# First layer of a macaron block: tokens loaded transposed as well, mean taken out by a constant product, reciprocal deviation put into the gates, order written out

## The chip, the cores and the metric

One core of one Trainium2 chip runs the whole kernel. The time is that of one execution on the device in microseconds (us), all of the kernel in one launch; of several runs the median counts. TensorE (PE) multiplies matrices, VectorE (DVE), ScalarE (ACT) and GpSimd (POOL) work on tiles in the core's own memory, SyncE (SP) issues the DMAs. Each engine takes its instructions in one fixed order and waits for other engines on semaphores.

## The reference

1024 tokens of 512 numbers pass three layers, all in float32:

```
x = x + 0.5 * FFN(LN(x));  x = x + Attention(LN(x));  x = x + 0.5 * FFN(LN(x))
LN(x) = (x - mean) / sqrt(var + 1e-5)
FFN(y): scores = y Wr^T (64 experts); gates = softmax of the 16 highest, others 0
        h = y A^T (64 experts x 16); out = (h * gate) B * 2
```

The attention has 32 heads over four sequences of 256 tokens, causal, and takes most of the time. The change concerns the first FFN.

## The kernel before, in words

The tokens lie in eight tiles of 128; two tiles make a pair. The first FFN, `ffn("f1", late=True)` from L274, works pair by pair in a fixed rhythm of generators. For a pair, `prepare` (L312) takes mean and variance on VectorE (`norm_stats`, L88), the root on ScalarE (L97), the reciprocal on VectorE (L101), writes the normed tile on ScalarE (L111), and turns it with eight 128x128 transposes on TensorE (`turned_x`, L114, ptx_f), which ScalarE copies to fxT_f (L321). Then come sums of quarters of it on VectorE (fxs_f, L171), the routing product against wr_sb (pr_f, L338) and `gates` (L282): the two highest groups of eight, an exponential on ScalarE (L301) and a division.

`hidden` (L348) multiplies a pair with A, `back` (L455) the gated result with B. Both are written as seven products of quarter matrices (Strassen's scheme, `seven`, L197) whose results are added on VectorE or copied on ScalarE (L367 to L371). Sums of quarters of A and B (at_f, bt_f; L191) are made once, on VectorE and POOL. `gated` (L378) multiplies the hidden values by their gates on POOL; `turned` (L409) turns the result with four groups of four transposes (pth_f, L441) and copies (L442). Pair 2's is turned by VectorE's 32x32 transposes and DMAs instead (`move`, L390), and ScalarE copies what comes back (L418). `back` adds to x on VectorE.

What sets the order: the program makes its calls in an order of its own, and a scheduler places the instructions on each engine from that; only the few marked `keep_in_program_order` are bound. The hidden products of pairs 0 and 1 are interleaved; from pair 2 on, the hidden products of one pair alternate with the back products of the pair before. SP's queue loads x0, x1, wr, two blocks of a, x2, x3, two blocks of a, x4 to x7, b, the first attention weights (L705 to L720, L227 to L250). Beside the pairs POOL makes sums of the attention's weights (L653). The normed tokens for the attention (`norm_pair`, ptx_a) are made behind each pair's back products. TensorE is kept busy from the start by 14 products of zeros (L86). The second FFN uses the same functions with `late=False`.

Of the kernel before, what the change touches and what calls it, by code (L numbers as in the profile page):

```python
# [14 lines left out]
P = 128  # L15
# [12 lines left out]
EPS = 1e-5  # L28
MASKED = -1e30
# [4 lines left out]
def macaron_kernel(  # L34
    ctx: ExitStack,
    tc: tile.TileContext,
    x_in: bass.AP,
    wq: bass.AP,
# [31 lines left out]
    load_x((0, 1))  # L70
    wr_sb = const.tile([P, DC, E], F32, tag="wr", name="wr_sb")
    nc.sync.dma_start(wr_sb, wr_t.rearrange("(c p) e -> p c e", p=P))
# [4 lines left out]
    nc.gpsimd.memset(eps, EPS)  # L77

    warm = const.tile([P, 1], F32, tag="warm", name="warm")
    nc.scalar.activation(warm, eps, AF.Sqrt)  # L80

    zeros = const.tile([P, P], F32, tag="zeros", name="zeros")
    nc.vector.memset(zeros, 0.0)
    idle = ps_s.tile([P, 512], F32, tag="s", name="idle")
    for _ in range(14):
        nc.tensor.matmul(idle[:, 0:P], lhsT=zeros, rhs=zeros, start=True, stop=True)  # L86

    def norm_stats(ts, name):  # L88
# [7 lines left out]
        std = small.tile([P, n], F32, tag="std", name=f"std_{name}")  # L96
        nc.scalar.activation(std, mv[:, :, 1], AF.Sqrt, bias=eps)  # L97
        minus = small.tile([P, n], F32, tag="minus", name=f"minus_{name}")
        nc.scalar.mul(minus, mv[:, :, 0], -1.0)
        rstd = small.tile([P, n], F32, tag="rstd", name=f"rstd_{name}")  # L100
        nc.vector.reciprocal(rstd, std)  # L101
# [5 lines left out]
    def normed(pool, ts, name, made=None):  # L107

        made = made or [pool.tile([P, D], F32, tag="xn", name=f"xn_{name}_{t}") for t in ts]
        for t, xn, (rstd, bias) in zip(ts, made, norm_stats(ts, f"{name}_{ts[0]}")):  # L110
            nc.scalar.activation(xn, x[:, t, :], AF.Identity, bias=bias, scale=rstd)  # L111
        return made
# [114 lines left out]
    def load_experts(scope, name, side, eng, between):  # L227
# [7 lines left out]
        at = pool.tile([P, 3, 2, 512], F32, tag="at", name=f"at_{name}")  # L235
        for i, kn in enumerate(((0, 0), (1, 0), (1, 1), (0, 1))):
            c, e = a_block(*kn)
            nc.sync.dma_start(a_sb[:, c, e], a_v[:, c, e])
            if i % 2:
                between(i // 2)  # L240
        for k in range(2):
            c = slice(4 * k, 4 * k + 4)
            nc.sync.dma_start(b_sb[:, c, :], b_v[:, c, :])
        every = [(k, n) for k in range(2) for n in range(2)]
# [4 lines left out]
        def keep():  # L249
# [6 lines left out]
            lambda: right_sums(eng, a_t3, *a_of, late=nc.gpsimd),  # L256
            lambda: right_sums(nc.gpsimd, b_t3, *b_of),
# [16 lines left out]
    def ffn(name, pairs, a_sums, b_sums, after, late, aside=None):  # L274


        with ExitStack() as scope:
# [4 lines left out]
            def gates(n, ps):  # L282
# [29 lines left out]
            def prepare(pair):  # L312
# [21 lines left out]
                gate = []  # L334
                for i, t in enumerate(pair):
                    ps = ps_mm.tile([P, 512], F32, tag="mm", name=f"pr_{name}_{t}")
                    for c in range(DC):
                        nc.tensor.matmul(  # L338
                            ps[:, :E],
                            lhsT=xt[:, i, c, :],  # L340
                            rhs=wr_sb[:, c, :],
                            start=(c == 0),
                            stop=(c == DC - 1),
                        )
                    gate.append(gates(f"{name}_{t}", ps))
                gated_by.append(gate)

            def hidden(pair, left, hgs):  # L348
# [14 lines left out]
                def read(r, ps):  # L363
# [4 lines left out]
                    elif adds:  # L368
# [4 lines left out]
                steps = STEPS_LATE if late and pair in pairs[:2] else STEPS  # L373
                if late and pair == pairs[1]:
                    steps = [steps[i] for i in (0, 1, 2, 4, 3, 5, 6)]
                yield from seven(product, read, f"ph_{n}", steps)
# [13 lines left out]
            def move(pair, hg):  # L390
# [5 lines left out]
                for i in range(2):  # L396
# [4 lines left out]
                    for t in range(4):  # L401
# [3 lines left out]
                        )  # L405
                for i in range(2):
                    nc.sync.dma_start(hg[:, i], moved[:, i].rearrange("p t x -> p (t x)"))

            def turned(pair, hg):  # L409
                n = f"{name}_{pair[0]}"  # L410
                hs = work.tile([P, 3, 4, P], F32, tag="hs", name=f"hs_{n}", bufs=1)
                if pair in by_dma:
# [3 lines left out]
                    s1, s2, s4 = (hs[:, i] for i in range(3))  # L416
                    for i in range(2):
# [4 lines left out]
                    for to, a, b, op in (  # L422
# [6 lines left out]
                    return {  # L429
                        "M1": a11, "M2": a12, "M3": s4, "M4": a22, "M5": s1, "M6": s2, "M7": a21  # L430
                    }
# [3 lines left out]

                for i, j in ((0, 0), (1, 0), (1, 1), (0, 1)):
                    pool, tag = (ps_t, "pt") if i or j else (ps_s, "s")
                    pt = pool.tile([P, 4, P], F32, tag=tag, name=f"pth_{n}_{i}_{j}")
                    for c in range(4):
                        cc = j * 4 + c  # L440
                        nc.tensor.transpose(pt[:, c, :], hg[:, i, cc * P : (cc + 1) * P], ident)  # L441
                    nc.scalar.copy(hgT[:, i, j * 4 : j * 4 + 4, :], pt)  # L442
# [8 lines left out]
                return {  # L451
                    "M1": a11, "M2": a12, "M3": s4, "M4": a22, "M5": s1, "M6": s2, "M7": a21
                }
# [26 lines left out]
            tokens = prepare(pairs[0])  # L480
            take(tokens, 1)
            yield
            take(tokens, 1)
            yield
            if late:
                second = prepare(pairs[1])
                take(second, 1)
            take(tokens, 1)
            a_right = a_sums()
            for u in range(n + 1):  # L490
                if u == 1 and late:
                    hid = ahead
                else:
                    hid = hidden(pairs[u], lefts[u], hgs) if u < n else iter(())
                tokens = prepare(pairs[u + 1]) if u + 1 < n else iter(())
                behind = after(work, pairs[u - 2]) if u > 1 else iter(())
                if u == 0 and late:

                    take(hid, 3)
# [1174 lines left out]
```

## Time and profile before

| | |
|---|---|
| median of 3 runs | 1114.08 us (1113.94 to 1115.47) |
| span of the profiled execution, first to last instruction | 1112.0 us |
| what the median has beyond that span | 2.1 us |
| TensorE busy | 1101.3 us, 99% |
| VectorE, GpSimd, ScalarE busy | 819.4, 626.1, 439.8 us |
| first hidden product of the first FFN starts | 10.23 us |
| first product of the attention starts | 126.53 us |

No time of the profiled execution other than its span is listed, so the median stands beside it. In the rows of the profile "L354" is a line of the kernel above, "ph_f<-a_f,fxT_f" what is written and read, "x8" the number of records, of which a matmul here has two and a transpose one. The brackets at a row's end give how long the engine stood idle ahead of it and which instruction ended that. TensorE's stretches list what it did; a chain of waits follows the last instruction back to what released it.

### The profile page before, as it was taken

What the parts mean: (1) busy time and instruction counts of PE and PEld (TensorE: products, weight loads), DVE (VectorE), ACT (ScalarE), POOL (GpSimd) and SP (SyncE); (2) the same over time, 40 slices, a digit from 0 to 9 for tenths busy, and PEclk for the clock granted to TensorE, in tenths of its full rate; (3) what the DMA queues carried; (4) which work ended last, traced back from release to release, by engine and by line L of the source; (5) the groups of instructions that cost most, each with busy time, mean ns of one, the idle gap of its engine ahead of it and who ended that gap; (6) DMA issues with size and microseconds to landing.
All of it is one profiled execution on the core that took longest, in us unless ns stands there. A gap on an engine that the chain in (4) does not pass through costs nothing.

```text
span 1112.0 us, 21021 instructions
## 1 busy us (share of the span) xinstructions
PE 1101.3 (99%) x6770; PEld 970.0 (87%) x6770; DVE 819.4 (74%) x2242; ACT 439.8 (40%) x1320; POOL 626.1 (56%) x870
## 2 busy tenths in 40 slices
PE   9999999999999999999999999999999999999998
PEld 6666888899999999999999999999899999995667
DVE  4554677678778778778778878878888978866543
ACT  4453424444544544544544544444452000106410
POOL 4814588736887887788788778878632000002120
PEclk9999999999999999999999999999999999999999
DMA  9221120157756756756656656756798998752331
GB/s 329 93 70 45 29 68 11 33 143 202 204 140 182 203 159 182 204 149 185 204 154 183 197 162 169 212 151 184 204 325 304 346 337 261 253 200 77 96 94 39
DMA packets 203774, 188.45 MB, mean 169 GB/s; under 512 B 74128, under 2 KB 166032, under 8 KB 203408
## 3 DMA queue, kind: packets, MB, share of 16 engines
q1 hardware_dynamic: 203664, 187.11, 56.2%
q8 instruction: 54, 0.88, 0.3%
q14 instruction: 56, 0.46, 0.1%
HBM read 117.18 MB, written 69.86 MB: 168 GB/s over the span
## 4 chain that ended last, share of the span: by engine, by line
PE 90%; DVE 3%; POOL 2%; ACT 1%; issue 1%; DMA 1%; SPq 0%; POOLq 0%; DVEq 0%
PE po_M L1196 15%; PE pqk_c L772 8%; PE po_f L461 8%; PE pqk_b L772 8%; PE pqk_d L772 8%; PE ph_f L354 7%; PE pa L1297 5%; PE ps L1221 5%; PE pv_c L871 5%; PE pqk_a L772 4%; PE pv_b L871 4%; PE ps L1220 2%; PE pa L1304 2%; PE pv_d L871 2%; PE pv_e L871 2%; PE pv_a L871 2%
## 5 line engine op out<-in xcount | busy, mean ns | idle before, releaser
L384 POOL TENSOR_TENSOR hg_f<-hg_f,gate_f 128x512 f32<-128x512 f32 x32 | 35.6, 1124 | 254.4 <-ACT gate_f L309 151.3
L1196 PE MATMUL po_M<-or_M,ol_M 128*128 128x128 f32 x1456 | 164.7, 275 | 0.0
L1196 PEld LDWEIGHTS po_M<-or_M,ol_M 128*128 128x128 f32 x1456 | 163.7, 192 | 0.1
L653 POOL TENSOR_TENSOR wqk_M<-wqk_M 128x128 f32<-128x128 f32 x320 | 141.5, 457 | 12.1
L653 POOL TENSOR_TENSOR wqk_M<-wqk_M,wqk_M 128x512 f32<-128x512 f32 (+1 forms) x64 | 107.1, 1683 | 45.4 <-DMA wqk_M<-in_wkv 16.5
L789 DVE TENSOR_TENSOR qk<-qk,pqk_d 128x512 f32<-128x512 f32 x210 | 116.3, 559 | 20.7 <-PE pqk_d L772 16.8
L1241 ACT ACTIVATE s<-s,least 128x128 f32<-128x128 f32 (+1 forms) x256 | 114.1, 448 | 40.5 <-DVE least L1229 35.6
L1259 ACT ACTIVATE pn<-s,arden 128x128 f32<-128x128 f32 x220 | 94.1, 428 | 47.7 <-DVE arden L1250 43.3
L772 PE MATMUL pqk_c<-xop,wqk_M 128*128 128x256 f32 x448 | 111.4, 380 | 0.1
L772 PE MATMUL pqk_d<-xop,wqk_M 128*128 128x256 f32 x420 | 108.2, 381 | 1.2 <-DVE qk L789 1.1
L772 PE MATMUL pqk_b<-xop,wqk_M 128*128 128x256 f32 x420 | 102.9, 379 | 0.0
L1096 DVE TENSOR_TENSOR ol_M<-ol_M 128x512 f32<-128x512 f32 x104 | 77.3, 744 | 22.6 <-DMA ol_M<-left 21.8
L1229 DVE CUSTOM_DVE_ANT_0 s<-ps,mask 128x128 f32<-128x128 f32 (+1 forms) x256 | 80.9, 353 | 16.3 <-PE ps L1221 12.3
L789 DVE TENSOR_TENSOR qk<-qk,pqk_c 128x256 f32<-128x256 f32 (+1 forms) x112 | 59.5, 531 | 40.5 <-PE pqk_c L772 36.4
L1311 ACT COPY attn<-pa 128x256 f32<-128x256 f32 x128 | 47.4, 371 | 100.6 <-PE pa L1304 87.9
L772 PEld LDWEIGHTS pqk_c<-xop,wqk_M 128*128 128x128 f32 x448 | 79.0, 191 | 8.7 <-ACT qk L821 1.2
L789 DVE TENSOR_TENSOR qk<-qk,pqk_b 128x512 f32<-128x512 f32 x105 | 71.4, 680 | 20.7 <-PE pqk_b L772 19.9
L772 PEld LDWEIGHTS pqk_b<-xop,wqk_M 128*128 128x128 f32 x420 | 74.9, 191 | 7.5
L772 PEld LDWEIGHTS pqk_d<-xop,wqk_M 128*128 128x128 f32 x420 | 73.0, 191 | 9.1 <-DVE qk L789 2.9
L1297 PE MATMUL pa<-pT,vbuf 128*128 128x256 f32 x256 | 76.4, 380 | 0.8 <-ACT pT L1287 0.5
L1221 PE MATMUL ps<-qk 128*128 128x256 f32 x256 | 76.5, 380 | 0.0
L653 POOL TENSOR_TENSOR wv_M<-wv_M 128x128 f32<-128x128 f32 x160 | 70.6, 458 | 3.8
(192 smaller groups left out, 2355.0 us busy)
## 6 DMA issues: line engine op xcount, KB each, us to landing
ol_M<-left SPq DMA_DIRECT2D x52, 512.0 KB, 5.6
moved<-s SPq DMA_DIRECT2D x440, 48.0 KB, 1.8
pT<-moved SPq DMA_DIRECT2D x110, 192.0 KB, 2.9
wv_M<-in_wkv SPq DMA_DIRECT2D x64, 128.0 KB, 2.7
wqk_M<-in_wq SPq DMA_DIRECT2D x64, 128.0 KB, 2.3
wqk_M<-in_wkv SPq DMA_DIRECT2D x64, 128.0 KB, 2.5
wo<-in_wo SPq DMA_DIRECT2D x16, 512.0 KB, 4.6
left<-attn SPq DMA_DIRECT2D x16, 512.0 KB, 3.3
```

Of the source, the lines that this page charges most:

```text
L354: nc.tensor.matmul(ps, lhsT=left[m][:, c, :], rhs=a_right[m][:, c, :], start=first and c == 0, stop=c == 1, skip_group_check=True,)
L461: nc.tensor.matmul(ps[:, 0:256], lhsT=left[m][:, c, :], rhs=b_right[m][:, c, :], start=first and c == 0, stop=c == 3, skip_group_check=True,)
L653: return nc.gpsimd.tensor_tensor(to, a, b, ALU.subtract)
L772: nc.tensor.matmul(ps[:, i * S : (i + 1) * S], lhsT=right[m][n], rhs=xop[OUTER[m]][:, INNER[n]], start=first and i == 0, stop=True, skip_g ...
L789: nc.vector.tensor_tensor(to, of, ps, ALU.add)
L871: nc.tensor.matmul(ps[:, i * S + t * P : i * S + (t + 1) * P], lhsT=xop[OUTER[m]][:, INNER[n], t * P : (t + 1) * P], rhs=right[m][n], star ...
L1196: nc.tensor.matmul(banks[at // 2][:, cols : cols + P], lhsT=lhsT, rhs=rhs, start=k % 4 == 0 and g == 0 and at % 2 == 0 and t == 0, stop=Tr ...
L1221: nc.tensor.matmul(ps[:, P : 3 * P], lhsT=qT[:, P : 2 * P], rhs=kT, start=True, stop=True)
L1229: nc.vector.tensor_tensor_reduce(out=s[:, cols], in0=ps[:, cols], in1=mask_f[:, cols], scale=-SCALE, scalar=-TAKEN, op0=ALU.add, op1=ALU.m ...
L1241: nc.scalar.activation(s[:, cols], s[:, cols], AF.Exp, bias=least[:, i : i + 1], scale=-1.0, accum_out=den[:, i : i + 1],)
L1259: nc.scalar.mul(pn[:, :, i : 2 * i + 1, :].rearrange("p k t c -> p t k c"), s[:, cols].rearrange("p (t k c) -> p t k c", k=4, c=32), rden[ ...
L1297: nc.tensor.matmul(po[:, 0 : 2 * P], lhsT=v_of(p, j, 2 * b), rhs=of[:, 0:2], start=True, stop=False,)
```

## The change

The host gives the tokens a second time, transposed (x_t, one block per pair). The first FFN loads these raw and takes the mean out of them: for pair 0 by eight matmuls with a constant 1/512 whose result VectorE subtracts, for the others by a diagonal matrix of the means from VectorE, one 128x256 matmul and one subtraction. Routing and hidden products take the tokens without the mean but not divided by the deviation; the reciprocal deviation goes into the exponential's scale and into the gates. It is computed by an addition on VectorE and a power of -0.5 on POOL, also for the attention's pairs 0 and 1; the root stays for its pairs 2 and 3 and for the second FFN.

With that, transposes, copies and normed tiles of the first FFN go. Five products of the constant stand where 14 of zeros stood. SP's queue now has pair 0 transposed, the four blocks of a, x2, x3, pair 1 transposed, x0, x1, wr, b, x4 to x7, the attention's first weights, pair 2 transposed, the stores of a and b, pair 3 transposed. The sums of a and b are split between VectorE and POOL. The order on TensorE, VectorE, ScalarE and POOL through the first FFN is written out: a clock counts TensorE's time (`goes_on`), and work of other engines is put in when its time comes (`later`). Pair 0's hidden products now come first, alone; then those of pair 1, which alternate with the back products of pair 0 in the same way as later pairs. The cut diff:

```diff
     wr_sb = const.tile([P, DC, E], F32, tag="wr", name="wr_sb")
...
 
...
+    halves = const.tile([P, 2], F32, tag="halves", name="halves")
...
 
...
-    zeros = const.tile([P, P], F32, tag="zeros", name="zeros")
-    nc.vector.memset(zeros, 0.0)
-    idle = ps_s.tile([P, 512], F32, tag="s", name="idle")
-    for _ in range(14):
-        nc.tensor.matmul(idle[:, 0:P], lhsT=zeros, rhs=zeros, start=True, stop=True)
-
...
+    nc.scalar.activation(warm, eps, AF.Exp)
+
+    every = const.tile([P, P], F32, tag="every", name="every")
+    nc.vector.memset(every, 1.0 / D)
+    idle = ps_t.tile([P, 512], F32, tag="pt", name="idle")
+    for _ in range(5):
+        nc.tensor.matmul(idle[:, 0:P], lhsT=every, rhs=every, start=True, stop=True)
+
...
+        if whole == "root":
+            std = small.tile([P, n], F32, tag="std", name=f"std_{name}")
+            nc.scalar.activation(std, mv[:, :, 1], AF.Sqrt, bias=eps)
+            nc.vector.reciprocal(rstd, std)
+        else:
+            nc.vector.tensor_scalar_add(rstd, mv[:, :, 1], EPS)
+            nc.gpsimd.tensor_tensor(rstd, rstd, halves[:, 0:n], ALU.pow)
+        if whole is None:
+            return mv, rstd
         minus = small.tile([P, n], F32, tag="minus", name=f"minus_{name}")
         nc.scalar.mul(minus, mv[:, :, 0], -1.0)
-        rstd = small.tile([P, n], F32, tag="rstd", name=f"rstd_{name}")
-        nc.vector.reciprocal(rstd, std)
+        if not whole:
+            return minus, rstd
         bias = small.tile([P, n], F32, tag="bias", name=f"bias_{name}")
...
             c, e = a_block(*kn)
             nc.sync.dma_start(a_sb[:, c, e], a_v[:, c, e])
-            if i % 2:
-                between(i // 2)
+            between(i)
         for k in range(2):
             c = slice(4 * k, 4 * k + 4)
             nc.sync.dma_start(b_sb[:, c, :], b_v[:, c, :])
+        between(4)
...
 
         return (
-            lambda: right_sums(eng, a_t3, *a_of, late=nc.gpsimd),
-            lambda: right_sums(nc.gpsimd, b_t3, *b_of),
+            lambda: right_pieces(a_t3, *a_of),
+            lambda: right_pieces(b_t3, *b_of),
...
+                gate, den, rden = each("gate", E, 4), each("den"), each("rden")
+                for i, ps in enumerate(scores):
+                    nc.vector.scalar_tensor_tensor(
+                        gate[i],
+                        left2[i],
+                        TAKEN,
+                        ps[:, E : 2 * E],
+                        ALU.is_equal,
+                        ALU.mult,
+                        accum_out=den[i],
+                    )
+                for i in range(2):
+                    nc.vector.reciprocal(rden[i], den[i])
+                for i in range(2):
+                    nc.vector.tensor_scalar(
+                        gate[i], gate[i], rden[i], rstd[:, i : i + 1], ALU.mult, ALU.mult
+                    )
+                gated_by.append(gate)
...
+            def prepare_raw(pair):
+
+                n = f"{name}_{pair[0]}"
+                xt = raw(pair)
+                mv, rstd = norm_stats(pair, n, None)
+                diag = work.tile([P, 2, P], F32, tag="mean", name=f"diag_{n}")
+                for i in range(2):
+                    nc.vector.tensor_scalar(
+                        diag[:, i], ident, mv[:, i, 0:1], float(D), ALU.mult, ALU.mult
+                    )
+                yield
+                ps = ps_s.tile([P, 512], F32, tag="s", name=f"pm_{n}")
+                mean = ps[:, 0 : 2 * P].rearrange("p (j t) -> p j t", j=2)
+                nc.tensor.matmul(mean, lhsT=every, rhs=diag, start=True, stop=True)
+                yield
+                nc.vector.tensor_tensor(
+                    xt, xt, mean.unsqueeze(2).to_broadcast([P, 2, DC, P]), ALU.subtract
+                )
+                xs = work.tile([P, 4, 2, P], F32, tag="fxs", name=f"fxs_{n}")
+                lefts.append(left_of(xt, xs))
+                yield
+                for scores in route(pair, xt):
+                    yield
+                yield from gates(pair, scores, rstd)
...
+                for c in range(DC):
+                    nc.tensor.matmul(
+                        ps[:, 0:P], lhsT=every, rhs=firsts["xt"][:, i, c], start=c == 0, stop=c == DC - 1
+                    )
+                return ps
...
+            def first_tile(i, ps):
+
+                to = firsts["xt"][:, i]
+                nc.vector.tensor_tensor(
+                    to, to, ps[:, 0:P].unsqueeze(1).to_broadcast([P, DC, P]), ALU.subtract
+                )
...
-                    steps = [steps[i] for i in (0, 1, 2, 4, 3, 5, 6)]
-                yield from seven(product, read, f"ph_{n}", steps)
+                steps = STEPS_LATE if late and pair == pairs[0] else STEPS
+                def later(r, ps):
+                    reads.append(lambda: read(r, ps))
+
...
-                if u == 1 and late:
-                    hid = ahead
-                else:
-                    hid = hidden(pairs[u], lefts[u], hgs) if u < n else iter(())
-                tokens = prepare(pairs[u + 1]) if u + 1 < n else iter(())
+                a_right, pieces = a_sums()
+                xt = firsts["xt"] = raw(pairs[0])
+                written_out = ExitStack()
+                written_out.enter_context(tc.manual_schedule(engines=FRONT))
+                means = [first_mean(pairs[0], i) for i in range(2)]
+                for i in range(2):
+                    first_tile(i, means[i])
+                xs = work.tile([P, 4, 2, P], F32, tag="fxs", name=f"fxs_{name}")
+                left = left_of(xt, xs)
+                lefts.append(left)
+                reads = []
+                hid = hidden(pairs[0], left, hgs, reads)
+
+                def readings(n):
+                    for _ in range(n):
+                        reads.pop(0)()
+
+                routed = route(pairs[0], xt)
+                take(hid, 3)
+                readings(1)
+                pieces[0](nc.vector)
+                take(hid, 1)
+                pieces[1](nc.vector)
+                readings(2)
...
+                readings(1)
+                scores = next(routed)
+                readings(2)
+                rstd = norm_stats(pairs[0], f"{name}_0", None)[1]
+                take(hid, 1)
+                readings(1)
+                take(routed, 1)
+                take(tokens, 2)
+                take(hid, 1)
+                readings(1)
+                made = gates(pairs[0], scores, rstd)
+                later(0.6, take, made, 2)
+                later(2.2, take, made, 1)
+                b_right, pieces = b_sums()
+                for i, piece in enumerate(pieces):
+                    later(1.5 + 1.2 * i, piece, (nc.gpsimd, nc.vector)[i % 2])
+                later(2.5, lambda: gate_of(0))
+                clock[0] = 0.0
...
+                        for _ in range(k):
+                            goes_on(next(turning_u, 0.0))
+
+                    later(clock[0] + 0.1, take, behind, 1)
+                    if pairs[u - 1] in by_dma:
+                        later(clock[0] + 2.0, turns, 1)
+                    for i in range(7):
+                        take(hid, 1)
+                        goes_on(1.72)
+                        if i == 2 and u == 1:
+                            routing(own)
+                        if i == 5:
+                            later(clock[0], take, tokens, 1)
+                        if i == 3 and u > 1:
+                            take(behind, 1)
+                            goes_on(0.9)
+                            later(clock[0] + 4.0, take, behind, 1)
+                        if pairs[u - 1] not in by_dma:
+                            turns({3: 3, 4: 2}.get(i, 0))
+                    later(clock[0] + 0.8, gate_of, u)
+                    if pairs[u] in by_dma:
+                        moving = move(pairs[u], hgs[pairs[u]])
+                        for at in (5.4, 7.2, 9.0):
+                            later(clock[0] + at, take, moving, 1)
+                    if u == 1:
+                        aside(later, clock[0] + 1.0)
+                    steps = back(pairs[u - 1], left, b_right)
+                    for i in range(7):
+                        take(steps, 1)
+                        goes_on(1.72)
+                        if i == 1 and u + 1 < n:
+                            take(tokens, 1)
+                            later(clock[0] + 0.5, take, tokens, 1)
+                            goes_on(0.43)
+                        if i == 4 and u + 1 < n:
+                            routing(tokens)
+                    take(steps, 1)
+                behind = after(work, pairs[n - 2])
+                left = {}
+                for step in turned(pairs[n - 1], hgs[pairs[n - 1]], left):
+                    goes_on(step)
+                later(clock[0] + 1.5, take, behind, 1)
+                steps = back(pairs[n - 1], left, b_right)
+                for i in range(7):
+                    take(steps, 1)
+                    goes_on(1.72)
+                    if i == 4:
+                        take(behind, 1)
+                        goes_on(0.9)
+                take(steps, 1)
+                goes_on(100.0)
+                written_out.close()
+            else:
+                tokens = ready(pairs[0])
+                take(tokens, 1)
+                yield
+                take(tokens, 1)
+                yield
+                take(tokens, 1)
+                a_right = a_sums()
...
-        experts = load_experts(
-            scope, "f1", "right", nc.vector, lambda i: load_x(range(4, NT) if i else (2, 3))
...
+        def between(i):
+            if i == -1:
+                for k in (0, 2):
+                    nc.sync.dma_start(
+                        raw_tile((0, 1))[:, 0, k : k + 2], xt_in[0][:, 0, k : k + 2]
+                    )
+                nc.sync.dma_start(raw_tile((0, 1))[:, 1], xt_in[0][:, 1])
+            elif i == 4:
+                load_x(range(4, NT))
+            elif i == 3:
+                load_x((2, 3))
+                nc.sync.dma_start(raw_tile((2, 3)), xt_in[1])
+                load_x((0, 1))
+                nc.sync.dma_start(wr_sb, wr_t.rearrange("(c p) e -> p c e", p=P))
+
...
+        def beside(later, time):
+            ones = [one for name in FIRST_SUMS for one in weights["v", 0][2][name]]
+            for i, one in enumerate(ones):
+                later(time + 0.7 * i, one)
+            later(time, experts[2])
```

## The prediction

> **What bounds the kernel now.** I read the busy shares first, then the chain of work that ended last, then TensorE's timeline over the first layer, then what feeds it.
>
> ```profile
> PE 1101.3 (99%) x6770; PEld 970.0 (87%) x6770; DVE 819.4 (74%) x2242; ACT 439.8 (40%) x1320; POOL 626.1 (56%) x870
> PE 90%; DVE 3%; POOL 2%; ACT 1%; issue 1%; DMA 1%; SPq 0%; POOLq 0%; DVEq 0%
> ```
>
> The reader is to see that TensorE is the bound, nearly everywhere. So the change is worth what it takes from TensorE's own work, from its standstills, and from the time before its first useful product. After the first layer both kernels issue the same instructions in the same order on every engine, but for one pair of attention matmuls put 5 us earlier; whatever the first layer gains or loses therefore arrives at the end as a shift.
>
> ```profile
> 1.05 5.71 PE L86 MATMUL idle<-zeros 128*128 128x128 f32 x28 [1.05 <-DVE zeros L83]
> 7.09 1.27 PE L118 MATMUL ptx_f<-ident,xn_f 128*128 128x128 f32 x8 [0.33 <-ACT xn_f L111]
> 8.39 2.00 PE L338 MATMUL pr_f<-wr_sb,fxT_f 128*128 128x64 f32 x16
> 10.23 3.65 PE L354 MATMUL ph_f<-a_f,fxT_f 128*128 128x512 f32 x8
> ...
> 16.45 1.10 PE L354 MATMUL ph_f<-at_f,fxs_f 128*128 128x512 f32 x2 [0.85 <-DVE gate_f L304]
> ...
> 45.54 1.99 PE L461 MATMUL po_f<-b_f,hgT_f 128*128 128x256 f32 x8 [0.84 <-ACT hgT_f L442]
> ...
> 56.01 3.60 PE L354 MATMUL ph_f<-a_f,fxT_f 128*128 128x512 f32 x8
> ...
> 126.53 0.61 PE L871 MATMUL pv_a<-wv_M,xop 128*128 128x128 f32 x4
> ```
>
> Columns: start, us, line, x records. This is TensorE in the first layer: warm-up, transposes, routing, first hidden product at 10.23, third pair's hidden from 56.01, first attention product at 126.53. I set these three marks against the changed order. One product of the seven takes 1.72 (8 records in 3.65 are two of them), four transposes 0.44, routing of a tile 0.86, a 128x256 matmul 0.43. By these rows 10.23 to 56.01 holds 43.2 us of work and 2.6 of standing still; 56.01 to 126.53 holds 69.0 and 1.5.
>
> ```profile
> 42.04 0.58 ACT L442 COPY hgT_f<-pth_f 128x512 f32<-128x512 f32 x1 [1.56 <-PE pth_f L441]
> 42.65 1.28 ACT L301 ACT_TABLE_LOAD   x1
> 43.94 0.55 ACT L301 ACTIVATE pr_f<-sc_f,nmax_f 128x64 f32<-128x64 f32 x2
> 44.44 1.05 ACT L442 COPY hgT_f<-pth_f 128x512 f32<-128x512 f32 x2
> ```
>
> On ScalarE the exponential's table load stands ahead of the copy that TensorE's 0.84 at 45.54 waits for. It is the only one of the eight loads of the front that a standstill of TensorE ends on.
>
> **The change, part by part.** All sums are against the profiled execution: span 1112.0, and the median 1114.08 lies 2.1 above, which I add at the end.
>
> *Start.* The five warm-up matmuls are 10 records 0.213 apart: until 3.2. The mean's eight matmuls need the transposed tile; x0 (256 KB, first in the queue) landed at 3.4, so 3.0 to 3.5. Before, records came 0.213 apart until about 5.6 and 0.111 apart after, though the granted clock stands at 1.00 in the rows throughout. The first tile's mean is 8 records, until 5.1; the second's until 6.0 (half of it at the fast spacing) or 6.8 (none). VectorE's subtraction of 128x512 out of PSUM (0.68 by the addition of L367) ends at 5.9. The first block of a needs 1.0 MB through a queue that had moved 1.1 MB when it landed at 8.1 before: 5.9 to 6.6. First hidden product: 6.1 to 6.8, I take 6.4 against 10.23, 3.8 earlier. But two routings (1.7) that were done by then are now still to come.
>
> *TensorE's work.* Gone after 10.23 are 24 transposes, 8 for each of pairs 1 to 3 (0.87 a pair); new is one 128x256 mean matmul for each (0.43). From the first product to the third pair's: 43.2 + 1.7 - 2 x 0.87 + 2 x 0.43 = 44.0. From there to the attention: 69.0 - 0.87 + 0.43 = 68.6.
>
> *Standstills that go.* 0.85 at 16.45 (VectorE had the second sum of a, 1.20 us, behind the landing at 13.75): the last block of a now lands some 3.4 earlier, since x2, x3 and wr go behind it, and its sums start at about 10.4; at most 0.3 stays. 0.84 at 45.54: no load stands there any more.
>
> *Standstills that come.* Routing weights are now behind 4 MB; at the 390 GB/s of the queue's later stretch they land at 15 to 16 and the first routing is due at 15: 0 to 1.0. The gates of pair 0 on POOL (4 x 1.06) end at about 30.7, the first transposes of its products are due at 30: 0 to 0.5. I take 0.8 in all. Third pair at 6.4 + 44.0 + 0.8 = 51.2, against 56.01.
>
> In the second stretch pair 2's gated products are moved by DMA:
>
> ```profile
> 74.59 1.25 DVE L397 STREAM_TRANSPOSE hgB_f<-hg_f 128x1024 f32<-128x1024 f32 x1 [0.80 <-POOL hg_f L384]
> 73.36 4.25 SPq L402 DMA_DIRECT2D moved_f<-hgB_f  x8
> 77.86 3.56 SPq L407 DMA_DIRECT2D hg_f<-moved_f  x2
> ```
>
> From the second transpose's end (75.84) to the last landing (about 85.0) are 9.2. In the written order the transposes come behind a 128x1024 subtraction (1.23) and four sums (0.4 each) of pair 3, and end 11.5 after pair 2's hidden products; the products are back at 21.3 (the landing takes 3.9 of it). ScalarE has the two copies that wait for them (L559 of the changed kernel, 1.04 each by L418) ahead of the copy (0.58) that frees pair 3's hidden accumulator, and TensorE's fifth product of pair 3 waits for that: due 22.2 (14.4 of back products, four of 1.72, 0.87 of transposes), freed 23.4 with a handover, a standstill of 1.2. The last pair's fourth transpose group waits for a PSUM buffer's copy: 0.45. To these I add 0.8 of small waits, of some 2 that the trace of before has without names, since in-order queues keep such. Second stretch: 68.6 + 2.45 = 71.05, end at 122.3, 4.2 ahead of 126.53.
>
> *Edits at nothing.* ScalarE loses 16 copies and activations and five table loads of 1.28; beyond the one named, it idled, and gains TensorE nothing. The sums of a and b, split between VectorE and POOL: POOL's six of 2.37 ran from 16.38 to 30.5; now four, with VectorE taking the others at 1.2. Cover: VectorE works 26.6 of the 45.8 us; without it each sum of a would cost its 1.2. The transposed tokens are 2 MB more in SP's queue and b lands some 5 us later, but its first product is due at 37. The stores of a and b now stand in SP's queue ahead of pair 3's transposed tokens, which are due 25 us later. The attention's first weight loads wait for the same late products of pair 3 in both; POOL's sums on them ended at 117.3, 9.2 before their use, and shift along. The Sqrt load for the attention's third pair comes early, ahead of an instruction that waits anyway.
>
> *pow on POOL, 128x2, six times:* no row shows it. Below: a memset of 128x1 (0.10); above: 128x1024 (2.37). Nearest in size is the memset; I take 0.3. Each goes ahead of gates or of xop: the first two have 3 us and more of slack, the one for attention pair 0 1.5, the one for pair 3 stands ahead of pair 2's gating, thus on the move above. At 2.37 they would cost 0 + 0 + 0.9 + 2.1 + about 0.5 = 3.5.
>
> *Skill, table loads.* The trace has 1.28 for a load, and the next activation starts 0.01 later. The Trainium skill ("ScalarE: Activation LUTs", What ACT_TABLE_LOAD costs) adds a drain of about 1.4, 2.7 a switch. By that five switches fewer would free 13 us of ScalarE instead of 6.4; for the time it makes no difference, and the row decides.
>
> *Skill, clock.* The spacing above halves at 5.6, 4.5 after the first matmul. The Trainium skill ("TensorE: Matmul & The Clock Gate", What's actually happening) has a free-running window of about 3.4 us that must be filled with activity; it speaks against five warm-up matmuls with gaps behind them. By it the first products could run at half speed until 9.8, a loss of 1.7.
>
> **Rivals.**
>
> A, more: the 1.2 and the unnamed 0.8 do not come, and wr lands in time. Lead 4.2 + 2.0 + 0.5 = 6.7: 1107.4. For it: TensorE's stretches of before stand still only 4%. Against: ScalarE's order is fixed.
>
> B, swallowed. The first products run cold, at 0.213 spacing for the 4.5 us that before needed (half of 4.5 = 2.2), or pow is slow (up to 3.5): lead 0.7 to 2.0, about 1112.6. For it: gaps between warm-up and first product that before did not have. Against: before, the fast spacing came at 5.6 and held through gaps of 0.33.
>
> C, slower. The written order ties pair 3's hidden products to pair 2's move: ScalarE cannot pass the L559 copies, and every us that the move is late is a us of TensorE. Price one for one. Lead is 4.2 with a landing at 21.3 after pair 2's products; it is gone if the landing is at 25.5, and 2.2 slower than before at 27.7, that is, if VectorE's transposes end at 18 instead of 11.5. For it: they stand behind gating on POOL, sums and gates in one fixed queue. Against: VectorE is half idle there (38 of 70.5). About 1117.
>
> D, nothing moves: the first layer ends earlier, but POOL's or the DMA's attention weights pace the rest. Against: the 9.2 of slack, which shifts too. Would give about 1113.5.
>
> **How the numbers follow.** Forecast 0.62, A 0.12, B and D 0.16, C 0.10. The likeliest: 1112.0 - 4.2 + 2.1 = 1109.9; its own range is 1108.3 to 1111.8. About 0.2% (2.2 us) is what a measurement here can tell from no change, so faster means under 1111.85. Faster 0.62 + 0.12 = 0.74, within 0.16, slower 0.10. The range takes in A and half of B: 1106.8 to 1113.6.
>
> **What would show it.** First hidden product at 6.1 to 6.8; its first products 1.72 each, not 3.4; third pair's hidden from 51 to 51.5; a standstill of about 1 at pair 3's fourth hidden step, ended by ScalarE; first attention product at 122 to 122.7; the rest as long as before. I am wrong if the pow rows are over 1 us, if the clock is late, if a wait that I put at nothing shows in TensorE's list, or if the stretch behind the first layer has another length.

## The result, and the profile after

The changed kernel takes 1119.28 us (median of 5, 1117.26 to 1121.69) against 1115.20 in the same series (5, 1113.94 to 1115.81): 1.0041 times as long, 95% interval 1.0028 to 1.0054. It is slower, by 0.4%; I forecast 1109.9 and gave slower a chance of 0.10. The profiled execution is the fastest of the five, 1117.26, with a span of 1115.5.

Shares of the page, and TensorE's timeline (start, us, line, then the idle time ahead of a row and who ended it):

```profile
PE 1098.6 (98%) x6742; PEld 967.5 (87%) x6742; DVE 836.8 (75%) x2260; ACT 419.7 (38%) x1275; POOL 627.2 (56%) x875
PE 89%; DVE 5%; POOL 2%; DMA 1%; issue 1%; ACT 1%; SPq 0%; POOLq 0%; DVEq 0%
```

```profile
6.98 1.96 PE L490 MATMUL ph_f<-a_f,fxT_f 128*128 128x512 f32 x4 [0.95 <-DMA a_f<-in_a_t]
...
20.38 1.96 PE L490 MATMUL ph_f<-at_f,fxs_f 128*128 128x512 f32 x4 [2.43 <-DVE hg_f L503]
...
36.90 0.66 PE L583 MATMUL pth_f<-ident,hg_f 128*128 128x128 f32 x4 [1.37 <-POOL hg_f L521]
...
57.58 3.60 PE L490 MATMUL ph_f<-a_f,fxT_f 128*128 128x512 f32 x8
...
105.16 1.99 PE L602 MATMUL po_f<-bt_f,hs_f 128*128 128x256 f32 x8 [1.46 <-DVE x L614]
...
129.57 0.59 PE L1059 MATMUL pqk_a<-xop,wqk_M 128*128 128x256 f32 x2
```

TensorE does less work (1098.6 against 1101.3) and the first useful product does come 3.25 earlier. But three waits that were not there before stand in the list, and VectorE's part of the chain has grown from 3% to 5%. Third pair: 57.58 against 56.01. Attention: 129.13 (129.57 less 0.44 for the attention matmuls moved ahead) against 126.53, so 2.6 lost where I had 4.2 won. Both stand still 0.28 for the vbuf addition nine us later, at 135.86 before and 138.45 after, again 2.6 apart. From there to the end the two profiled executions differ by another 0.9 (976.2 and 977.0); executions of the kernel before differ by 1.9 among themselves (1113.94 to 1115.81), so this is not told from noise.

Who does VectorE wait for? The first wait's additions (L503) were ready at 17; ahead of them in VectorE's queue stand the two diagonal products of the next pair. First VectorE, then POOL:

```profile
16.86 0.22 DVE L119 TENSOR_SCALAR rstd_f<-mv_f 128x2 f32<-128x2 f32 x1
17.00 2.64 DVE L391 TENSOR_SCALAR diag_f<-ident,mv_f 128x128 f32<-128x128 f32 x2
19.56 1.40 DVE L503 TENSOR_TENSOR hg_f<-hg_f,ph_f 128x512 f32<-128x512 f32 x2
```

```profile
17.01 2.35 POOL L217 TENSOR_TENSOR at_f<-a_f,at_f 128x1024 f32<-128x1024 f32 x1
```

The six products of this kind, by themselves (min/median/max in ns):

```profile
L391 DVE TENSOR_SCALAR diag_f<-ident,mv_f x6: 274/281/2444, 17.0 to 74.7; 128x128 f32<-128x128 f32 x6
```

Of the 2.64 the first product has 2.44, until 0.08 after POOL's sum has ended (19.36), and the second its own 0.28. So one product waited for the whole of POOL's sum. The same kernel has more of it. A sum of 128x256 (L197) takes 1.20 at 24.95 beside a sum on POOL, and its neighbours, with POOL idle, 0.42. POOL's four gatings of pair 0 take 6.22, and 4.11 for pair 1, where VectorE makes no sums of B. It is the first two that are slow, 2.19 and 2.04, beside VectorE's two sums; the others take their 1.05:

```profile
L521 POOL TENSOR_TENSOR hg_f<-hg_f,gate_f x4: 1050/1544/2193, 30.6 to 35.8; 128x512 f32<-128x512 f32 x4
30.68 1.22 DVE L217 TENSOR_TENSOR bt_f<-b_f 128x1024 f32<-128x1024 f32 x1
31.93 1.97 DVE L217 TENSOR_TENSOR bt_f<-b_f,bt_f 128x1024 f32<-128x1024 f32 x1
```

The attention's eight sums of 128x256 (L197) take 5.6 from 99.17: five take 0.42 each, and the last three, beside POOL's gating, 1.16 to 1.27. So they hold up the additions to x for which TensorE waits 1.46. In the kernel before, the same eight sums (L171) stand where POOL is idle, and take 0.42 each. First the changed kernel, then the one before:

```profile
100.95 3.54 POOL L521 TENSOR_TENSOR hg_f<-hg_f,gate_f 128x512 f32<-128x512 f32 x3 [8.55 <-ACT hg_f L507]
101.22 2.36 DVE L197 TENSOR_TENSOR xop<-xop 128x256 f32<-128x256 f32 x2
103.50 1.27 DVE L197 TENSOR_TENSOR xop<-xop,xop 128x256 f32<-128x256 f32 x1
```

```profile
95.88 1.43 DVE L171 TENSOR_TENSOR xop<-xop 128x256 f32<-128x256 f32 x4
98.98 4.61 POOL L384 TENSOR_TENSOR hg_f<-hg_f,gate_f 128x512 f32<-128x512 f32 x3 [7.32 <-DVE hg_f L367]
```

The Trainium skill has this (SBUF - State Buffer, Who interferes with whom): VectorE and GpSimd share a pair of ports, held for a whole instruction; VectorE takes it with two inputs in SBUF, or with forms such as the plain tensor_scalar that use both ports for one input. With an input in PSUM it does not. I did not weigh this page, and it speaks against the change: before, the sums of the tokens read the transposes out of PSUM, the memory that TensorE writes. There they stand beside a 2.37 sum on POOL and lose nothing, VectorE first, then POOL, both of the kernel before:

```profile
19.35 0.42 DVE L171 TENSOR_TENSOR fxs_f<-fxT_f,ptx_f 128x256 f32<-128x256 f32 x1 [1.14 <-ACT fxT_f L321]
19.81 0.42 DVE L171 TENSOR_TENSOR fxs_f<-fxs_f,ptx_f 128x256 f32<-128x256 f32 x1
```

```profile
18.69 2.37 POOL L191 TENSOR_TENSOR at_f<-a_f,at_f 128x1024 f32<-128x1024 f32 x1
```

Tokens loaded transposed lie in SBUF, the core's own memory, so their sums and the diagonals compete with POOL, and two of POOL's sums of B were put on VectorE in the same stretch.

Theory L: the three waits are this exclusion. Rivals: O, the written order just has too much ahead in its queues; D, late loads; W, TensorE's clock (the five executions of the result had a mean granted clock of 1.000 once, at 1117.26, and 0.997 or 0.998 four times, at 1117.81 to 1121.69; the kernel before had 1.000 in every execution made beside the experiments).

### The profile page after: what moved, and what is told of

Read it like the earlier page. It is cut to its first block, busy times and chain, and to the rows that moved or that the text cites. A ratio compares the mean times of both kernels' runs of the same rounds, so it can differ in the third digit from the quotient of the medians.

```text
span 1115.5 us, 20937 instructions
## 1 busy us (share of the span) xinstructions
PE 1098.6 (98%) x6742; PEld 967.5 (87%) x6742; DVE 836.8 (75%) x2260; ACT 419.7 (38%) x1275; POOL 627.2 (56%) x875
## 4 chain that ended last, share of the span: by engine, by line
PE 89%; DVE 5%; POOL 2%; DMA 1%; issue 1%; ACT 1%; SPq 0%; POOLq 0%; DVEq 0%
PE po_M L1483 15%; PE pqk_c L1059 9%; PE pqk_b L1059 8%; PE pqk_d L1059 7%; PE po_f L602 7%; PE ph_f L490 6%; PE pa L1584 5%; PE ps L1508 5%; PE pv_c L1158 5%; PE pqk_a L1059 4%; PE pv_b L1158 4%; PE ps L1507 2%; PE pa L1591 2%; PE pv_d L1158 2%; PE pv_a L1158 2%; PE pv_e L1158 2%
```

## The experiments

Each is the changed kernel with the edit shown. I compare by medians, and by the place of the vbuf wait (138.45 in the changed kernel, 135.86 before), which says how late the first layer was in the profiled execution.

**diag_act: the diagonals on ScalarE.**

```diff
-  nc.vector.tensor_scalar(diag[:, i], ident, mv[:, i, 0:1], float(D), ALU.mult, ALU.mult)
+  nc.scalar.mul(diag[:, i], ident, md[:, i : i + 1])     # md: mean times D, 128x2, on VectorE
```

> The changed kernel, but the two diagonal products of each later pair (128x128, mean times identity) are made on ScalarE instead of VectorE. Theory L (VectorE and POOL keep each other out while both read the core's memory: the two products took 2.64 us beside a 2.36 us sum on POOL): the additions behind them start at 17.2 instead of 19.56, TensorE's standstill of 2.43 at 20.38 falls to 0.3 or less, the end comes 2 us earlier. Rival O (the fixed order just puts too much work ahead, each product at its own 0.2 to 0.3): the standstill falls by 0.5 at most. Rival D (late loads): nothing moves. Rival W (the clock is low in most runs, by the short warm-up): the rows move as in L or O, the median does not.

The additions start at 16.83, the standstill of 2.43 is gone, the mark comes at 137.13. Median 1116.39 (10, ratio 1.0020, 1.0010 to 1.0029), and the clock is 1.000 in all ten. D and O fall as the cause of this wait. Only 1.3 of the 2.4 arrives at this place, the mark: a wait of 1.28 on ScalarE at pair 3's fifth product has come up, the one I had forecast at 1.2, and the waits on POOL are now one of 1.74.

**diag_accum: same engine, same place, other form.**

```diff
-  diag[:, i], ident, mv[:, i, 0:1], float(D), ALU.mult, ALU.mult
+  diag[:, i], ident, mv[:, i, 0:1], float(D), ALU.mult, ALU.mult, accum_out=unused[:, i : i + 1]
```

> The changed kernel, but VectorE's two diagonal products also write out their sum (a column nobody reads); same engine, same place, same data. Theory L in the form that the Trainium skill gives it (SBUF - State Buffer, Who interferes with whom): the accumulating form does not take the pair that POOL needs, so the two take some 0.3 to 0.5 each beside POOL's sum, the standstill of 2.43 falls to about 0.5 to 1.0. Rival O and rival D: the two stay at 2.6 or the standstill stays. If they stay at 2.6 although POOL is idle, they are slow by themselves.

VectorE, then POOL:

```profile
17.54 0.33 DVE L392 TENSOR_SCALAR_CACHE_REDUCE diag_f<-ident,mv_f 128x128 f32<-128x128 f32 x1
...
17.81 0.34 DVE L392 TENSOR_SCALAR_CACHE_REDUCE diag_f<-ident,mv_f 128x128 f32<-128x128 f32 x1
```

```profile
17.57 2.35 POOL L217 TENSOR_TENSOR at_f<-a_f,at_f 128x1024 f32<-128x1024 f32 x1
```

This is the cleanest of the runs: more work per instruction, the same data and order, POOL busy over both, and they take 0.33 and 0.34 instead of 2.44 and 0.28. The standstill is 0.40, the median 1116.96 (10, ratio 1.0020, 1.0011 to 1.0030). So here it is the form of the instruction that collides with POOL, not the load of VectorE, as the page says of the plain and the accumulating form.

**b_late: VectorE's sums of B behind the gating.**

```diff
-  later(1.5 + 1.2 * i, piece, (nc.gpsimd, nc.vector)[i % 2])
+  later(1.5 + 1.2 * i + 6.0 * (i > 0), piece, (nc.gpsimd, nc.vector)[i % 2])
```

> The changed kernel, but the last three of the four sums of B, two of them on VectorE, are put 6 us later in the written order, behind the gating of pair 0 on POOL. Theory L: the four gating products take 4.2 us instead of 6.22 (1.06 each as in the kernel before), TensorE's two waits on POOL at 34.87 and 36.90 (0.30 and 1.37) fall to 0.3 together; end 1.4 earlier. Rival O (the gates come late, at 30.6, and that is all): the gating stays at 1.5 a product and the waits stay.

POOL's gating of pair 0, of the changed kernel and of this one:

```profile
30.62 6.22 POOL L521 TENSOR_TENSOR hg_f<-hg_f,gate_f 128x512 f32<-128x512 f32 x4 [4.76 <-DVE gate_f L357]
```

```profile
31.95 4.11 POOL L521 TENSOR_TENSOR hg_f<-hg_f,gate_f 128x512 f32<-128x512 f32 x4 [6.22 <-DVE gate_f L357]
```

The gating starts later and ends earlier, both waits on POOL are gone. A new one of 0.90 stands at the next pair's mean, whose statistics are now behind a sum of B. The median, 1118.46 (6, ratio 1.0032, 1.0020 to 1.0044), is hardly below the changed kernel's: four of the six had a clock of 0.998 (the 2.43 is still in it). The two at 1.000 took 1116.23 and 1116.66. Its profiled execution is one of the four. There the product behind the standstill takes 3.65, where it takes 1.96 in the changed kernel's:

```profile
20.24 3.65 PE L490 MATMUL ph_f<-at_f,fxs_f 128*128 128x512 f32 x4 [2.43 <-DVE hg_f L503]
```

**xop_late: the attention's sums behind additions of the back products.**

```diff
-  later(clock[0] + 4.0, take, behind, 1)
+  later(clock[0] + (4.0 if u < n - 1 else 10.0), take, behind, 1)
```

> The changed kernel, but the attention's sums over its second pair (VectorE, seven of 128x256) are put 6 us later in the order, behind the first additions of pair 2's back products. Theories L and O both: the standstill of 1.46 at 105.16 goes, and the end comes 1.4 earlier; L also expects the sums, which took 0.8 to 1.3 each beside POOL's gating, to take 0.4 to 0.9 each where they now stand beside POOL's shorter 0.46 sums. If the 1.46 stays, it was not VectorE's queue.

Both theories missed what they share: the 1.46 goes, but 2.20 comes at 112. What L adds held: beside POOL's short sums of weights the eight sums take 0.56 to 0.73 each. That is still 4.9 in one piece, and the additions queued behind them are late again. Median 1121.72 (4, ratio 1.0064, 1.0049 to 1.0079). It shows something else, the columns being the stretch, its length, busy times and counts, with the granted clock third from the end:

```profile
20.00:22.00 2.00, 2.00 (x4) 1.00 (x5) 1.93 (x5) 0.59 (x1) 0.00 (x0) 0.72 1.06 390
22.00:24.00 2.00, 2.00 (x9) 1.48 (x8) 0.98 (x3) 0.00 (x0) 1.59 (x2) 0.50 1.13 329
24.00:26.00 2.00, 2.00 (x7) 1.23 (x7) 1.09 (x1) 0.00 (x0) 1.41 (x1) 0.93 1.09 272
```

Behind the standstill of 2.43 the granted clock is 0.72, then 0.50, then 0.93, and the first product takes 2.6 instead of 1.7. At half clock that is 1.1, 2.0 and 0.3 us, 3.4 in all. By my estimate that costs half of it, 1.7 of TensorE's work; b_late's row above shows the same 1.7. The two products behind the 2.20 are slow in the same way (2.7 and 2.6). All four executions had 0.997. That is W, though not at the start, where I had looked for it.

**again and fill: the clock alone.** again has no edit. fill:

```diff
   scores = next(routed)
+  for _ in range(5):
+      nc.tensor.matmul(scores[0][:, 256:512], lhsT=every, rhs=xt[:, 0, 0:2], start=True, stop=True)
```

> The changed kernel itself once more, for its clock. Theory W (after a standstill of TensorE of more than some 2 us the granted clock is at half for 2 to 4 us, in part of the executions): the standstill of 2.43 at 20 is in every one, and the mean granted clock is under 1.000 in most; those with 1.000 take about 1117.5, the others 1119 to 1122. Without W the clock is 1.000 or the times do not follow it.

> The changed kernel with five matmuls of 128x256 more (0.43 each, 2.15 in all, results read by nobody) behind the first routing product of pair 0, where TensorE stands still for 2.43. They delay nothing that VectorE does, so the next product starts at 20.4 as before. Theory W: the clock is 1.000 in all executions and the median falls to about 1117.5, 2 us under the changed kernel's own on the same chip, by work added. Theory L without W: no change, or slower by what the five take.

again: 1119.20 (5, ratio 1.0042, 1.0027 to 1.0056), clock 1.000 once (1117.65) and 0.997 or 0.998 four times (1118.39 to 1121.02). fill: 1117.91 (6, ratio 1.0031, 1.0019 to 1.0043), clock 1.000 six times; its next product starts at 20.12, as in again (20.13). So five useless matmuls keep the clock. The 1.3 between the two medians is not established by these intervals, which overlap.

**fill_two: two of the five.** The same edit with range(2).

> The changed kernel with two of the five added matmuls (0.86 in all), so that the standstill at 17.9 is cut from 2.43 to about 1.5 and nothing else moves. Theory W with a bound between 1.74 (the longest standstill of the kernel whose clock was 1.000 in all ten executions) and 2.2: the clock is 1.000 in all, the median 1117.9 as with five. If the clock counts TensorE's work over a longer stretch, not one standstill, some executions stay at 0.998.

A standstill of 1.52 is left, and the clock is 1.000 in all four. The median is 1118.92 (ratio 1.0039, 1.0024 to 1.0055), not 1117.9: its profile has 1.6 of waiting for blocks of A and 1.0 on ScalarE where fill has none and 0.4. Why those differ I did not settle, and by these pairs the clock's price in time is between 0.3 and 1.3. Within one kernel the executions with a lower clock can be set beside those at 1.000. For the changed kernel and again together, the six at 0.998 took 1.7 longer on the mean than the two at 1.000, and the two at 0.997 3.9 longer; the same difference for 0.998 is 2.3 in b_late, 1.0 in diag_accum and 0.7 in both_late below. That agrees with one fall of 1.7 for 0.998 and two for 0.997, as xop_late's profile has two; the samples are small.

**lock_free: all three.** diag_act, and

```diff
-  later(1.5 + 1.2 * i, piece, (nc.gpsimd, nc.vector)[i % 2])
+  later((1.5, 8.7, 9.9, 15.5)[i], piece, (nc.gpsimd, nc.vector)[i % 2])
...
-            yield
             for o in range(2):
+                yield
                 inner_sums(o, nc.vector)
...
   later(clock[0] + 4.0, take, behind, 1)
+  if u == n - 1:
+      later(clock[0] + 11.0, take, behind, 1)
```

> The changed kernel with the diagonal products on ScalarE, the two sums of B that VectorE makes put behind the gating of pair 0 (the second behind the next pair's statistics), and the attention's sums over its second pair put in two halves with additions of the back products between them. Theory L: of the kernel with the diagonal alone moved (1116.4), TensorE's waits of 1.74 (POOL's gating), 1.45 (VectorE's additions) and 0.17 go, and 0.2 of refilling with each: 3 to 4 us, 1112.4 to 1113.4, clock 1.000 throughout. Rival O (the order's queues are full anyway): a wait elsewhere takes their place, and the time stays over 1115.5.

1112.65 (10, ratio 0.9980, 0.9971 to 0.9989): 6.5 less than the changed kernel on the same chip, inside what L gave, and faster than the kernel before. Clock 1.000 in all ten, mark at 133.69, 4.8 earlier than the changed kernel's. TensorE's waits over the first 150 us (in total, times, longest):

```profile
PE ph_f L490 <- ACT hg_f L507: 1.1, 1, 1.1
PE idle L88 <- DVE every L85: 1.1, 1, 1.1
PE ph_f L490 <- DMA a_f<-in_a_t: 0.9, 1, 0.9
PE ph_f L490 <- DVE a_f L217: 0.7, 1, 0.7
```

None of the three is left, as L expected. POOL's four gatings of pair 0 take 1.05 to 1.06 each; of the attention's eight sums four stand ahead of POOL's gating and take 0.42 each, four beside its short sums, 0.56 to 0.67. Behind the first product the longest wait is now the forecast's own. For the 1.46 no run made the sums fast and left them in their place, so its cause rests on the rows above; lock_free also breaks up the queue.

**lock_free_copies, both_late, both_spread: that last wait.** In turn: ScalarE's copies of pair 2's products later; VectorE's sums of them later too; the attention's first four sums behind three additions.

```diff
-  later(clock[0] + 2.0, turns, 1)
+  later(clock[0] + 5.3, turns, 1)            # lock_free_copies
+  later(clock[0] + 9.6, turns, 1)            # both_late as well: a yield between copies and sums
...
-  later(clock[0] + 4.0, take, behind, 1)     # both_spread as well; 11.0 becomes 13.5
+  later(clock[0] + (4.0 if u < n - 1 else 10.0), take, behind, 1)
```

> As lock_free, and ScalarE's two copies of the moved products of pair 2 stand 3.3 us later in the order, behind the copy that frees pair 3's accumulator. The forecast's step (the copies hold that one up) says: the wait of TensorE on ScalarE of 1.28 at pair 3's fifth hidden product goes, 1.2 to 1.4 less than lock_free: 1111.0 to 1112.2. Rival: pair 2's sums on VectorE come later by as much, the back products wait for them, and nothing is gained.

> lock_free with ScalarE's copies of pair 2's moved products behind the copy that frees pair 3's accumulator, and now VectorE's four sums of them behind the additions of pair 3's hidden products too (in lock_free_copies they stood ahead and made TensorE wait 1.51). If the forecast's step and its successor are all that stood there, neither the 1.08 of lock_free nor the 1.51 comes: 1.1 to 1.3 less than lock_free, 1111.3 to 1111.6. Rival: the move itself is late and the back products wait for the sums instead: no better than 1112.6.

> both_late, with the attention's eight sums over its second pair put in two fours between the additions of pair 2's back products, the first four now behind three of these additions and not ahead of them. Theory L with queues: four such sums beside POOL take some 2.5 us, and the kernel with eight in one place (5.0 us) stood still for 2.20, so four are borne: no standstill over 0.5 behind the start but VectorE's wait for a block of A, clock 1.000 in all, 1.1 to 1.3 less than lock_free: 1111.2 to 1111.8. If a standstill of 1 to 2 comes up again at another place, these queues hold no more gain in this stretch and 1112.6 is the end of it.

lock_free_copies: 1114.09 (10, ratio 0.9993, 0.9984 to 1.0003). The wait on ScalarE is gone, but 1.51 on VectorE stands two products on: the rival. both_late: 1116.33 (11, ratio 1.0016, 1.0008 to 1.0025). Both are gone, but the attention's first four sums come late, two of them beside POOL's gating (1.28 and 1.16), the additions behind them are late, TensorE stands still 2.62, and the clock is 0.998 in eight of eleven. both_spread: 1112.94 (11, ratio 0.9987, 0.9978 to 0.9996), clock 1.000 in all, no standstill over 0.47 between the first product and the mark, which comes at 133.19. That is 0.5 earlier than lock_free, but the time is not below lock_free's 1112.65. So my expectation of 1.1 to 1.3 less failed. The waits behind the first product sum to 1.97 against lock_free's 2.59, as small ones of other names came up (0.38 on the additions to x, 0.36 for a block of A). Where the 0.5 at the mark went is not shown: the one profile has 1.3 of waits for the attention's moved scores that lock_free's does not list, and the two sets of executions overlap. lock_free has the lowest ratio of all, though the intervals of the two overlap.

## Why the prediction was wrong

- **Start**, taken as 6.4: 6.98. TensorE waited 0.95 for the first block of A behind the means. Mis-sized by 0.6.
- **TensorE's work** up to the third pair, 44.0: lock_free has 46.54 between its two marks (6.96 and 53.50), less 1.22 of listed waits, 45.3; the changed kernel has 50.60 less 4.87, 45.7. Part of it stands behind waits: the product at 6.98 takes 1.95 until the wait that follows, where others take 1.72. The rest I did not take apart. Mis-sized by 1.3 to 1.7.
- **Standstills that come**, 0.8: 4.87 (0.41 and 0.36 for blocks and sums of A, 2.43, 0.30 and 1.37). This is the step that failed. It was costed in "Edits at nothing" with "Cover: VectorE works 26.6 of the 45.8 us", that is by an engine's idle share, as if an instruction's time did not depend on what POOL does; the diagonal products had no term at all. Of the routing weights, which I gave 0 to 1.0, nothing came: the wait at that place was for the diagonals. For POOL's gates I gave 0 to 0.5; they were 1.67, since two of the four gatings took 2.19 and 2.04 beside VectorE's sums and not 1.06.
- **Second stretch**, 71.05: 71.55, right in sum by luck and wrong in its parts. The 1.2 on ScalarE is there in diag_act (1.28) and lock_free (1.08), but the changed kernel's list does not have it, and 1.46 stood there that I had not foreseen. In diag_act both stand.
- **pow**, taken as 0.3, is 0.69 to 0.72 for 128x2. It was hidden, as I had it.
- **Clock.** Rival B put it at the start. There the fast spacing of TensorE's records came in time with five matmuls, at 5.0 (at 6.0 before, and not at the 5.6 that I read); half speed until 9.8, which I had worked out from the skill's figure, is not what this trace shows. The clock fell later, behind the standstill of 2.43. The profiled execution (1117.26) had no fall, the other four had a mean clock of 0.997 or 0.998, and the 2.0 up to the median (1119.28) is about the price of one fall.
- **Rival C**, the one on the slower side, named ScalarE and the move (its 2.2 slower is 1116.3 from 1114.1, and not the 1117 given). Slower came mostly by three other places, where VectorE and POOL hold each other up, and by the clock.
- The shift behind the first layer held within about 1 us: 2.6 at the attention's start, 2.6 at the mark, 3.5 by the spans of the two profiled executions; for lock_free 2.17 at the mark and 2.06 by medians.

Put together, from 4.2 won to 2.6 lost: start 0.6, first stretch 5.8 (50.60 against 44.8, of which 4.1 are standstills), second 0.5. The medians are 4.1 apart; the other 1.5 is about what one fall of the clock costs.

## What to carry to other kernels

Before work is given to a half idle VectorE, look at what POOL does in the same stretch and where the operands lie: a sum of 128x256 with one input in PSUM ran beside POOL at its own 0.42, one with both in SBUF took 1.16 to 1.27 beside long instructions of POOL and slowed POOL too. A queue in fixed order turns one such instruction into a wait for all behind it, so small urgent additions belong ahead of bulk sums, and bulk sums are cut into pieces. TensorE's standstills of 2.2 to 2.6 us were in most executions followed by some 3.4 us at half clock, which their rows do not show, so a profile at full clock can flatter a kernel whose other executions fall.

## What the runs showed of the hardware

- The diagonal product of 128x128 took 0.28 alone, 2.44 when it started with a POOL sum of 2.35, and 0.33 there in the accumulating form.
- The holding up goes both ways: a gating of 1.06 on POOL took 2.19 and 2.04 beside VectorE's sums of B, and the second of these sums 1.97 instead of 1.22.
- The clock fell in part of the executions with a standstill of 2.20 to 2.62 (4 of 4, 4 of 6, 8 of 10, 8 of 11), and in none of those whose longest was 1.52 or 1.74 (4, 10). diag_accum does not fit well: 3 of 10 at 0.998, while its profiled execution, at 1.000, has none over 1.45. The others were not profiled, so this stays open. The Trainium skill (TensorE: Matmul & The Clock Gate, What's actually happening) has the clock fall after an idle window of about 3.4, and the window running free; that not every execution falls agrees with a free-running window, and the 3.4 at half clock with its length; that 2.20 to 2.62 were enough is less than the idle time that the page states.
